# A new order in the tail of a mixture-of-experts kernel, and results scattered to their tokens

## The chip, the cores and the metric

The kernel runs on one core of one Trainium2 chip. A core has a matrix engine (TensorE, PE in the profile, with its weight loads as PEld), a vector engine (VectorE, DVE), a scalar engine (ScalarE, ACT), a general engine (GpSimd, POOL) and a queue engine (SyncE, SP), which issues most of the DMA transfers. Every engine works through its own list of instructions in order and waits for the others by semaphores. The metric is the device time of one execution, in microseconds (us). Three executions of the kernel before took 3097.17, 3097.98 and 3100.47 us; the median is 3097.98 us.

## The reference

Eight images of 256 channels and 32 x 32 pixels pass through two layers. The first is a deformable convolution-attention with a learned position bias. Its result is added to x. For the second, every image is a list of 1024 tokens of 256 numbers:

```python
t = _to_tokens(x)                                  # (8, 1024, 256)
n = _ln_t(t)
query = einsum('bnd,de->bne', n, q_weight)
t = t + einsum('bnm,bmd->bnd', sigmoid(einsum('bnd,bmd->bnm', query, n)), n)
tokens = _ln_t(t)
probs = softmax(tokens @ router_w.T)               # 8 experts
rw, re = top_k(probs, 2); rw = rw / rw.sum(-1)
out = tokens
for e in range(8):
    y = gelu(tokens @ w1[e] + b1[e]) @ w2[e] + b2[e]
    out = out + combine[:, e] * y                  # combine: rw where e is one of the two, else 0
x = _from_tokens(t + out)
```

All of it is in float32. The kernel computes only the two chosen experts of a token.

## The kernel before

The images, called batches here, run one behind the other. For each of them the main loop at L1118 makes 64 turns, which compute the position bias (three small layers, `first_layer`, `second_layer`, `third_layer`) and the softmax of the first layer. That work keeps PE busy for most of the kernel. The other work is written as Python generators. Every `yield` is a place at which the main loop goes on with something else, so the order of the instructions on each engine is the order in which the generators are advanced; `in_order` (L76) fixes it, except for the scatters at L793, which may move between the fixed POOL instructions on either side of them.

The generators of a batch are:

- `prep`: normalisation, offsets and sampling for the next batch.
- `attention` (L606): `upper` and `rest`. `rest` ends the softmax, forms the tokens `x1`, the normalised `tt` and `tn`, the queries (`to_query`), and then the sigmoid attention in `slots` (L714, with `ap`, `sg`, `vp`). `finish` normalises each pair of token tiles into `ut`, adds `ut` to `x1`, stores the sum in the memory tensor `xu`, and computes the router's logits.
- `route` (L812), from `rest`: the two experts of each token, their weights, and for each token and choice a row number, `slot`. Rows of one expert stand together and start at a tile border. A tile has 128 rows, in the last batch 256.
- The 16 scatters (L793): one indirect DMA for each of 8 token tiles and 2 choices writes rows of `ut` to the memory tensor `xs` at their `slot`. POOL issues them.
- `experts` (L911): per round, 256 rows. It fetches `xl` from `xs`, turns it with four transposes into `xg`, multiplies by the first weights (`hp`), applies Gelu (`ht`), multiplies by the second weights (`yp`), adds the bias into `yt` and stores that in the memory tensor `ys` (L951). The weights come by DMA from the expert number, which SP loads into a register (L931, L932). It has 12 rounds of two tiles for batches 0 to 6, with four weight loads a round, and 15 rounds of one tile for batch 7, with two.
- `combine` (L991), 22 steps: it fetches `xu` (`xc`), gathers for each token tile and choice the rows of `ys` at `slot` by an indirect DMA (`gs`, L1019), adds each gathered tile times its weight to `xc` (L1011), turns the sums back to channels (L1002, L1004) and stores them in `out` (L1005).

Tiles named by `low(...)` share 12 buffers, those by `psum(...)` two PSUM banks. In the main loop, `mix` decides when a third of a round of `experts` runs, for the batch two before the current one. After the last turn (L1175) the tail begins: `mains` holds the rest of batch 7's attention, `mixtures` the rounds of batch 6, `sums` the `combine` of batch 5. The loop is short:

```python
while mains:
    advance(mains)
    if sorted_ or not attending and n % 2:
        whole()
    sorted_ = sorted_ or sorting
    step(sums)
    n += 1
while mixtures:
    whole()
    step(sums)
```

`whole()` runs three steps, that is one round. `attending` holds while `slots` runs and while `route` runs, `sorting` while `route` runs. Batch 6's `combine` is appended to `sums` when its last round is done, and from there on it takes one step for each scatter of batch 7; what is left of it goes between batch 7's rounds. Batch 7's `combine` runs alone at the end.

Of the kernel before, what the change touches and what calls it, by code (L numbers as in the profile page):

```python
# [16 lines left out]
P = 128  # L17
# [14 lines left out]
def tiles_of(slots):  # L32
# [14 lines left out]
_CST = [  # L47
    ("ident", 128), ("gavg", 128), ("base", 128), ("basef", 128),
    ("gq", 1), ("cx", 1), ("cy", 8), ("rev", 8),
    ("one", 1), ("before", 128), ("full", 8), ("upto", E * E), ("tiles", TILES), ("form", 12),  # L50
]


# [50 lines left out]
def tile_conv_attn_hybrid(ctx: ExitStack, tc: tile.TileContext, x, par, qw, w1, w2_, cst, out):  # L104
# [118 lines left out]


    xss = [nc.dram_tensor(f"xs{n}", [ROWS, C], F32, kind="Internal").ap() for n in range(2)]
    power = cpool.tile([P, 8], F32, name="power")
    nc.vector.memset(power, -0.5)
    sents = set()
# [377 lines left out]
    def attention(b, st, o, rt):  # L606
# [66 lines left out]
        def finish(q):  # L673
            mv = tiny[q % 2][:, 0:4].rearrange("p (u s) -> p u s", s=2)
            for u in range(2):
                statistics(x1[:, 2 * q + u, :], mv[:, u, :])
            by = yield from factors(mv, 2)
            normalize(x1, ut, 2 * q, by)
            yield
            tp = psum("bp").rearrange("p (k i) -> p k i", k=2)  # L680
            for k in range(2):
                for u in range(2):
                    nc.tensor.transpose(
                        tp[:, k, u * P : (u + 1) * P], ut[:, 2 * q + u, k * P : (k + 1) * P], ident
                    )
            un = low("un")
            nc.scalar.copy(un, tp)
            uns.append(un)
            yield
            pair = slice(2 * q, 2 * q + 2)  # L690
            nc.gpsimd.tensor_tensor(x1[:, pair, :], x1[:, pair, :], ut[:, pair, :], ALU.add)
            nc.sync.dma_start(out=xu.rearrange("(m p) c -> p m c", p=P)[:, pair, :], in_=x1[:, pair, :])
            if q % 2:
                lq = psum("lq")
                for k in range(2):
                    for p_ in (q - 1, q):
                        nc.tensor.matmul(
                            lq[32 * p_ : 32 * p_ + 32, 0:Q], lhsT=rw[:, k, :], rhs=uns[p_][:, k, :],
                            start=(k == 0), stop=(k == 1), tile_position=(0, 32 * p_),
                        )  # L700
                rows = slice(32 * q - 32, 32 * q + 32)
                nc.scalar.copy(lqs[rows], lq[rows, 0:Q])
                yield
# [55 lines left out]
        def rest():  # L759
            nonlocal attending, sorting, ut, lqs  # L760
            for n, _ in enumerate(softmax(st, 1, 1, st["last"], o, psum)):
                if n == 1:
                    residual_bias(1)
                yield
            yield from to_query(1)
            ut = tokens("ut")
            lqs = low("lqs", (P, Q))
            attending = True

            for n, _ in enumerate(slots([(q, mp) for q in range(4) for mp in range(2 if q < 2 else 0, 4)], True)):  # L770
                if n % 3 == 0:
                    yield
                    others()
                yield
                others()
            attending = False
            while finishing:
                yield
                others()
            attending = sorting = True  # L780

            steps = route(lqs, rt, LARGE if b == NB - 1 else SMALL)
            for _ in range(5):
                while b < NB - 1 and turn % 2 == 0:
                    yield
                next(steps)
                yield
            attending = sorting = False

            xs, group = xss[b % 2], f"slots{b}"  # L790
            for n in range(16):
                m, c = divmod(n, 2)
                sent = nc.gpsimd.indirect_dma_start(  # L793
                    out=xs[:, :], out_offset=bass.IndirectOffsetOnAxis(ap=rt["slot"][:, c, m : m + 1], axis=0),
                    in_=ut[:, m, :], in_offset=None,
                )
                if n:
                    tc.declare_no_dep(sent.ins, group=group, reason="other slots")
                tc.add_to_no_dep_group(group, sent.ins)
                sents.add(sent.ins.name)  # L800
                if n == 1:
                    run(steps)
                yield
            rt.update(xs=xs, xu=xu)
            mixtures.append((b, experts(b, rt)))
# [105 lines left out]
    def experts(b, rt):  # L911
# [2 lines left out]

        several = LARGE // slots_
        rounds = -(-tiles_of(slots_) // several)
        yv = dram.tile([rounds * LARGE, C], F32, name=f"ys{slots_}")
        rows, tokens_, first, second = {}, {}, {}, {}

        def at(t):  # L920
            return slice(t * LARGE, (t + 1) * LARGE)

        def fetch(t):
            rows[t] = low("xl")
            nc.sync.dma_start(out=rows[t], in_=xs[at(t), :].rearrange("(s p) c -> p s c", p=P))  # L925

        def weights(t, pool, width, w, name):
# [11 lines left out]
        for n in range(rounds + 2):  # L939
            if n >= 2:  # L940
                f2, ht = second.pop(n - 2), tokens_.pop(n - 2)
                yp = psum("yp").rearrange("p (s c) -> p s c", s=2)
                for s in range(2):
                    for f in range(2):
                        nc.tensor.matmul(  # L945
                            yp[:, s, :], lhsT=ht[:, f, s * P : (s + 1) * P],
                            rhs=f2[:, s * several // 2, f * C : (f + 1) * C], start=(f == 0), stop=(f == 1),
                        )
                yt = low("yt")
                nc.vector.tensor_tensor(yt, yp, f2[:, 0:several, 2 * C :].to_broadcast([P, 2, C]), ALU.add)  # L950
                nc.sync.dma_start(out=yv[at(n - 2), :].rearrange("(s p) c -> p s c", p=P), in_=yt)  # L951
            if n == rounds + 1:
                break
            yield
            if n + 2 < rounds:
                fetch(n + 2)
            if n < rounds:
                second[n] = weights(n, w2pool, 3 * C, w2_, "w2")
            if 1 <= n <= rounds:
                f1, xg = first.pop(n - 1), tokens_[n - 1]  # L960
                hp = psum("hp").rearrange("p (f i) -> p f i", f=2)
                for f in range(2):
                    for u in range(several):
                        us = slice(u * slots_, (u + 1) * slots_)
                        for k in range(2):
                            nc.tensor.matmul(  # L966
                                hp[:, f, us], lhsT=f1[:, u, k * C + f * P : k * C + (f + 1) * P], rhs=xg[:, k, us],
                                start=(k == 0), stop=(k == 1),
                            )
                tokens_[n - 1] = ht = low("ht")  # L970
                for f in range(2):
                    for u in range(several):
                        us = slice(u * slots_, (u + 1) * slots_)
                        nc.scalar.activation(  # L974
                            ht[:, f, us], hp[:, f, us], AF.Gelu, bias=f1[:, u, 2 * C + f : 2 * C + f + 1]
                        )
            if n + 1 < rounds:
                first[n + 1] = weights(n + 1, w1pool, 2 * C + 2, w1, "w1")
            yield
            if n < rounds:  # L980
                xl = rows.pop(n)
                tp = psum("tp").rearrange("p (k i) -> p k i", k=2)
                for k in range(2):
                    for s in range(2):
                        nc.tensor.transpose(tp[:, k, s * P : (s + 1) * P], xl[:, s, k * P : (k + 1) * P], ident)  # L985
                tokens_[n] = xg = low("xg")
                nc.scalar.copy(xg, tp)  # L987
            yield
        sums.append((b, combine(b, rt, yv)))

    def combine(b, rt, yv):  # L991
        xu, slot = rt["xu"], rt["slot"]
# [125 lines left out]
    for n in range(NB * TURNS):  # L1118
# [9 lines left out]
        if b == 0 and i in (8, 16):  # L1128
            nc.sync.dma_start(
                out=xss[i // 8 - 1].rearrange("(t p) c -> p t c", p=P),  # L1130
                in_=zero.unsqueeze(1).to_broadcast([P, ROWS // P, C]),
            )
        if i == 46:
            residual(b)
        coming_ = (n // 8 + 1) * 16
# [37 lines left out]
            side.finish()  # L1173
    logits(total - 1)
    mains.append((b, below))  # L1175
    n = sorted_ = 0
    while mains:
        advance(mains)
        if sorted_ or not attending and n % 2:
            whole()  # L1180
        sorted_ = sorted_ or sorting
        step(sums)
        n += 1
    while mixtures:
        whole()
        step(sums)
    while sums:
        step(sums)
# [47 lines left out]
def _constants():  # L1236
# [14 lines left out]
        "full": np.broadcast_to(SMALL * np.arange(8.0)[None, :], (P, 8)),  # L1251
        "upto": np.broadcast_to((np.arange(E)[None, :] <= np.arange(E)[:, None]).reshape(1, E * E), (P, E * E)),
        "tiles": np.broadcast_to(np.arange(TILES)[None, :], (P, TILES)),


        "form": np.array(
# [40 lines left out]
```

## Time and profile before

| | |
|---|---|
| median of three runs | 3097.98 us (3097.17 to 3100.47) |
| the profiled execution | 3097.26 us |
| its span, first to last instruction | 3095.5 us |
| PE busy | 2814.5 us, 91% |
| PEld busy | 1391.9 us, 45% |
| DVE busy | 1932.1 us, 62% |
| ACT busy | 1872.0 us, 60% |
| POOL busy | 1381.3 us, 45% |
| DMA moved | 311.22 MB, mean 101 GB/s |
| mean granted TensorE clock | 0.976 |

The profile is of one execution. Busy times say how long an engine worked, not whether anything waited for it; the share over the whole span is a mean over the long main loop and a tail of about 300 us that looks quite different. A group's line gives the line of the code, the engine, the operation, the tiles written and read, and what ended the idle time before it in square brackets. SPq is SP's queue of DMA instructions, and the time of such an instruction is that of issuing it, not of the transfer.

### The profile page before, as it was taken

How to read it: one execution, taken by the hardware profiler on the slowest of the kernel's cores; microseconds unless marked ns; L12 is line 12 of the kernel's file. 1: busy time of each engine (PE TensorE's matmuls, PEld its weight loads, DVE VectorE, ACT ScalarE, POOL GpSimd, SP SyncE). 2: the span in 40 equal slices, each digit the busy share in tenths (PEclk: the TensorE clock that was granted, in tenths of full speed). 3: DMA queues.
4: the chain of work that ended last, by engine and by line, in shares of the span. 5: the costliest groups of instructions: out<-in, count | busy, mean ns of one | idle time of the engine just before them, and what ended most of it. 6: DMA issues, size and time to landing. Idle time of an engine off the chain costs nothing. (4 is left out here: it accounts for less than half of the span.)

```text
span 3095.5 us, 51726 instructions
## 1 busy us (share of the span) xinstructions
PE 2814.5 (91%) x19592; PEld 1391.9 (45%) x19592; DVE 1932.1 (62%) x2968; ACT 1872.0 (60%) x2715; POOL 1381.3 (45%) x945
## 2 busy tenths in 40 slices
PE   3889998899999999999999999999999999998845
PEld 2223443344454454544445444544545444446634
DVE  4887668766765677656865667656776565652211
ACT  3676656666666657666676666666566666663211
POOL 2555334643354544545535463545435454451131
PEclk7999999999999999999999999999999999999968
DMA  2321111111373125512364124731256331645556
GB/s 85 106 46 35 22 28 43 47 37 26 99 215 86 45 62 161 180 47 57 88 190 134 48 59 112 210 91 44 63 150 188 91 75 38 188 124 166 169 179 188
DMA packets 428297, 311.22 MB, mean 101 GB/s; under 512 B 284432, under 2 KB 368656, under 8 KB 428048
## 3 DMA queue, kind: packets, MB, share of 16 engines
q1 hardware_dynamic: 415472, 273.14, 31.5%
q0 software_dynamic: 12288, 33.57, 3.5%
q8 instruction: 155, 2.54, 0.3%
q10 hardware_dynamic: 288, 1.20, 0.1%
q14 instruction: 94, 0.77, 0.1%
HBM read 239.93 MB, written 67.90 MB: 99 GB/s over the span
## 5 line engine op out<-in xcount | busy, mean ns | idle before, releaser
L477 POOL TENSOR_TENSOR h<-ta,nb 128x1024 f32<-128x1024 f32 x512 | 980.8, 1918 | 1187.3 <-PE h2p L490 956.0
L490 PE MATMUL h2p<-h,pr__101 64*64 64x512 f32 x8192 | 1011.4, 606 | 59.6 <-DVE h L498 31.4
L496 ACT ACTIVATE h<-h2p,pr__101 128x1024 f32<-128x1024 f32 x512 | 570.4, 1114 | 537.1 <-PE h2p L490 535.6
L498 DVE TENSOR_TENSOR h<-h2p,nc 128x1024 f32<-128x1024 f32 x512 | 625.5, 1222 | 296.6 <-PE h2p L490 283.7
L475 DVE TENSOR_TENSOR h<-ta,still 128x1024 f32<-128x1024 f32 x512 | 620.1, 1211 | 28.8 <-ACT still L464 26.4
L482 ACT ACTIVATE h<-h 128x1024 f32<-128x1024 f32 x512 | 537.7, 1050 | 9.3 <-POOL h L477 9.1
L490 PEld LDWEIGHTS h2p<-h,pr__101 64*64 64x64 f32 x8192 | 254.0, 132 | 575.1 <-issue 286.6
L517 PE MATMUL sim<-h,pr__101 128*32 128x512 f32 x4096 | 493.4, 599 | 0.0
L950 DVE TENSOR_TENSOR yt<-yp,w 128x512 f32<-128x512 f32 x99 | 68.5, 692 | 352.8 <-PE yp L945 312.4
L517 PEld LDWEIGHTS sim<-h,pr__101 128*32 128x32 f32 x4096 | 107.4, 109 | 361.5 <-issue 361.5
L723 PE MATMUL ap<-qt,tn 128*128 128x256 f32 x1024 | 251.0, 389 | 2.5 <-DVE x L745 1.0
L733 PE MATMUL vp<-tt,sg 128*128 128x256 f32 x1024 | 233.0, 381 | 3.5 <-ACT nc L459 3.3
L723 PEld LDWEIGHTS ap<-qt,tn 128*128 128x128 f32 x1024 | 184.9, 190 | 86.2 <-issue 41.7
L945 PE MATMUL yp<-w,ht 128*128 128x256 f32 x792 | 198.0, 394 | 21.4 <-ACT ht L974 8.1
L1019 POOL DMA_INDIRECT gs<-ys,slot x128 | 129.2, 1009 | 192.5 <-DMA xc<-xu 107.3
L966 PE MATMUL hp<-xg,w 128*128 128x128 f32 (+1 forms) x1464 | 202.0, 291 | 12.5 <-ACT xg L987 3.5
L733 PEld LDWEIGHTS vp<-tt,sg 128*128 128x128 f32 x1024 | 193.7, 190 | 36.5 <-ACT nc L459 5.0
L966 PEld LDWEIGHTS hp<-xg,w 128*128 128x128 f32 x1464 | 182.4, 193 | 54.0 <-issue 33.6
L745 DVE TENSOR_TENSOR x<-x,vp 128x512 f32<-128x512 f32 x64 | 44.0, 688 | 237.1 <-PE vp L733 237.1
L974 ACT ACTIVATE ht<-hp,w 128x128 f32<-128x128 f32 (+1 forms) x366 | 108.2, 376 | 133.3 <-PE hp L966 126.3
L741 ACT ACTIVATE sg<-ap 128x512 f32<-128x512 f32 x128 | 76.4, 597 | 160.4 <-PE ap L723 149.8
L945 PEld LDWEIGHTS yp<-w,ht 128*128 128x128 f32 x792 | 144.5, 193 | 56.5 <-ACT ht L974 13.7
(272 smaller groups left out, 2566.1 us busy)
## 6 DMA issues: line engine op xcount, KB each, us to landing
w<-in_w SPq DMA_DIRECT2D x183, 384.0 KB, 3.7
w<-in_w SPq DMA_DIRECT2D x183, 257.0 KB, 3.4
ta<-fd SPq DMA_DIRECT2D x128, 256.0 KB, 4.9
xl<-xs SPq DMA_DIRECT2D x99, 256.0 KB, 3.3
ys<-yt SPq DMA_DIRECT2D x99, 256.0 KB, 2.2
nb<-fd SPq DMA_DIRECT2D x128, 128.0 KB, 4.7
xb<-in_x SPq DMA_DIRECT2D x8, 1024.0 KB, 4.9
x<-in_x SPq DMA_DIRECT2D x8, 1024.0 KB, 7.5
```

What stands on the lines that cost most here:

```text
L475: nc.vector.tensor_tensor(h1, a, b, ALU.max)
L477: nc.gpsimd.tensor_tensor(h1, a, b, ALU.subtract)
L482: nc.scalar.activation(h1, h1, AF.Relu)
L490: nc.tensor.matmul(h2p[gs, r, :], lhsT=par_("w2")[rs, gs], rhs=h1[rs, g].rearrange("p y x -> p (y x)"), start=True, stop=True, tile_positi ...
L496: nc.scalar.activation(h2, h2p, AF.Relu, bias=par_("cb2"))
L498: nc.vector.tensor_tensor(h2.rearrange("p r (y x) -> p r y x", x=W), h2p.rearrange("p r (y x) -> p r y x", x=W), nc_.unsqueeze(3).to_broad ...
L517: nc.tensor.matmul(sim[32 * q : 32 * q + 32, :], lhsT=par_("z3")[:, 15 - m : 47 - m], rhs=h2s[2 * u + q // 2][:, q % 2, :], start=False, s ...
L723: nc.tensor.matmul(ap[:, u, :], lhsT=tn[:, k, m0 : m0 + P], rhs=qt[:, k, quarter(q)], start=(k == 0), stop=(k == 1),)
L733: nc.tensor.matmul(vp[:, i, :], lhsT=sgs[s][:, u, i * P : (i + 1) * P], rhs=tt[:, 2 * todo[n - 2 + s][1] + u, :], start=(s == u == i == 0) ...
L945: nc.tensor.matmul(yp[:, s, :], lhsT=ht[:, f, s * P : (s + 1) * P], rhs=f2[:, s * several // 2, f * C : (f + 1) * C], start=(f == 0), stop ...
L966: nc.tensor.matmul(hp[:, f, us], lhsT=f1[:, u, k * C + f * P : k * C + (f + 1) * P], rhs=xg[:, k, us], start=(k == 0), stop=(k == 1),)
L1019: nc.gpsimd.indirect_dma_start(out=got[m][:, c, :], out_offset=None, in_=yv[:, :], in_offset=bass.IndirectOffsetOnAxis(ap=slot[:, c, m : m ...
```

## The change

The change has three parts, all for the tail and the last batch.

In the tail's loop, rounds of batch 6 run at other steps: one step in three where attention is not running, one in nine where it is, and every step of `route`. After `route` the one-in-three rule holds again. `combine` of batch 6 no longer steps in this loop; only that of batch 5 does. In the loop that follows, `sums` takes two steps a round.

Batch 7's tokens carry a 257th number, the row at which their result is to be stored. For the first choice that is the number of the token, for the second the same plus 1024. `ut` has 257 columns in this batch; its last column is filled from new constants, and 1024 is added to it after the eight scatters of the first choice, which now all come before those of the second. The rows go to a memory tensor of their own, `xsl`. It is filled once, in batch 0, with zeros and, in the last column, with row numbers past the tokens, for the rows that no token takes.

Each round of batch 7 copies that column of its 256 rows into `ids`. Instead of storing `yt` in `ys`, it scatters `yt` with two indirect DMAs from POOL to `zs`, at `ids`. In place of `combine`, `add_up` reads the token sums and both choices' results in token order with 12 plain DMAs, four of them issued from ACT, then multiplies, adds, transposes and stores as before.

```diff
--- before.py
+++ after.py
@@ -47,7 +47,7 @@
 _CST = [
     ("ident", 128), ("gavg", 128), ("base", 128), ("basef", 128),
     ("gq", 1), ("cx", 1), ("cy", 8), ("rev", 8),
-    ("one", 1), ("before", 128), ("full", 8), ("upto", E * E), ("tiles", TILES), ("form", 12),
+    ("one", 1), ("before", 128), ("full", 8), ("upto", E * E), ("tiles", TILES), ("form", 12), ("token", 2 * N // P + tiles_of(LARGE) * LARGE // P),
 ]
 
 
@@ -223,6 +223,11 @@
 
 
     xss = [nc.dram_tensor(f"xs{n}", [ROWS, C], F32, kind="Internal").ap() for n in range(2)]
+
+    last_tiles = tiles_of(LARGE)
+    xsl = nc.dram_tensor("xsl", [last_tiles * LARGE, C + 1], F32, kind="Internal").ap()
+    zs = nc.dram_tensor("zs", [2 * N + last_tiles * LARGE, C], F32, kind="Internal").ap()
+    ids = cpool.tile([P, last_tiles, 2], I32, name="ids")
     power = cpool.tile([P, 8], F32, name="power")
     nc.vector.memset(power, -0.5)
     sents = set()
@@ -675,7 +680,7 @@
             for u in range(2):
                 statistics(x1[:, 2 * q + u, :], mv[:, u, :])
             by = yield from factors(mv, 2)
-            normalize(x1, ut, 2 * q, by)
+            normalize(x1, ut[:, :, 0:C], 2 * q, by)
             yield
             tp = psum("bp").rearrange("p (k i) -> p k i", k=2)
             for k in range(2):
@@ -688,7 +693,7 @@
             uns.append(un)
             yield
             pair = slice(2 * q, 2 * q + 2)
-            nc.gpsimd.tensor_tensor(x1[:, pair, :], x1[:, pair, :], ut[:, pair, :], ALU.add)
+            nc.gpsimd.tensor_tensor(x1[:, pair, :], x1[:, pair, :], ut[:, pair, 0:C], ALU.add)
             nc.sync.dma_start(out=xu.rearrange("(m p) c -> p m c", p=P)[:, pair, :], in_=x1[:, pair, :])
             if q % 2:
                 lq = psum("lq")
@@ -763,7 +768,11 @@
                     residual_bias(1)
                 yield
             yield from to_query(1)
-            ut = tokens("ut")
+            if b == NB - 1:
+                ut = t8.tile([P, 8, C + 1], F32, tag="t8", name="ut")
+                nc.vector.tensor_copy(ut[:, :, C], cst_("token")[:, 0:8])
+            else:
+                ut = tokens("ut")
             lqs = low("lqs", (P, Q))
             attending = True
 
@@ -787,9 +796,13 @@
                 yield
             attending = sorting = False
 
-            xs, group = xss[b % 2], f"slots{b}"
+            xs, group = xsl if b == NB - 1 else xss[b % 2], f"slots{b}"
             for n in range(16):
                 m, c = divmod(n, 2)
+                if b == NB - 1:
+                    c, m = divmod(n, 8)
+                    if n == 8:
+                        nc.vector.tensor_scalar(ut[:, :, C], ut[:, :, C], float(N), None, ALU.add)
                 sent = nc.gpsimd.indirect_dma_start(
                     out=xs[:, :], out_offset=bass.IndirectOffsetOnAxis(ap=rt["slot"][:, c, m : m + 1], axis=0),
                     in_=ut[:, m, :], in_offset=None,
@@ -914,14 +927,14 @@
 
         several = LARGE // slots_
         rounds = -(-tiles_of(slots_) // several)
-        yv = dram.tile([rounds * LARGE, C], F32, name=f"ys{slots_}")
+        yv = None if b == NB - 1 else dram.tile([rounds * LARGE, C], F32, name=f"ys{slots_}")
         rows, tokens_, first, second = {}, {}, {}, {}
 
         def at(t):
             return slice(t * LARGE, (t + 1) * LARGE)
 
         def fetch(t):
-            rows[t] = low("xl")
+            rows[t] = low("xl", (P, 2, xs.shape[1]))
             nc.sync.dma_start(out=rows[t], in_=xs[at(t), :].rearrange("(s p) c -> p s c", p=P))
 
         def weights(t, pool, width, w, name):
@@ -948,7 +961,16 @@
                         )
                 yt = low("yt")
                 nc.vector.tensor_tensor(yt, yp, f2[:, 0:several, 2 * C :].to_broadcast([P, 2, C]), ALU.add)
-                nc.sync.dma_start(out=yv[at(n - 2), :].rearrange("(s p) c -> p s c", p=P), in_=yt)
+                if b < NB - 1:
+                    nc.sync.dma_start(out=yv[at(n - 2), :].rearrange("(s p) c -> p s c", p=P), in_=yt)
+                for s in range(2 if b == NB - 1 else 0):
+                    sent = nc.gpsimd.indirect_dma_start(
+                        out=zs[:, :], out_offset=bass.IndirectOffsetOnAxis(ap=ids[:, n - 2, s : s + 1], axis=0),
+                        in_=yt[:, s, :], in_offset=None,
+                    )
+                    if n > 2 or s:
+                        tc.declare_no_dep(sent.ins, group="results", reason="other tokens")
+                    tc.add_to_no_dep_group("results", sent.ins)
             if n == rounds + 1:
                 break
             yield
@@ -983,10 +1005,38 @@
                 for k in range(2):
                     for s in range(2):
                         nc.tensor.transpose(tp[:, k, s * P : (s + 1) * P], xl[:, s, k * P : (k + 1) * P], ident)
+                if b == NB - 1:
+                    nc.vector.tensor_copy(ids[:, n], xl[:, :, C])
                 tokens_[n] = xg = low("xg")
                 nc.scalar.copy(xg, tp)
             yield
-        sums.append((b, combine(b, rt, yv)))
+        sums.append((b, combine(b, rt, yv) if b < NB - 1 else add_up(b, rt)))
+
+    def add_up(b, rt):
+
+        xu, got = rt["xu"].rearrange("(m p) c -> p m c", p=P), []
+        zv = zs[0 : 2 * N, :].rearrange("(c m p) d -> p c m d", c=2, p=P)
+        for q in range(4):
+            pair = slice(2 * q, 2 * q + 2)
+            xl, z0, z1 = low("xc"), low("z0"), low("z1")
+            nc.sync.dma_start(out=xl, in_=xu[:, pair, :])
+            nc.sync.dma_start(out=z0, in_=zv[:, 0, pair, :])
+            nc.scalar.dma_start(out=z1, in_=zv[:, 1, pair, :])
+            got.append((xl, z0, z1))
+        for q, (xl, *zc) in enumerate(got):
+            tp = psum("op").rearrange("p (k i) -> p k i", k=2)
+            for u in range(2):
+                for c in range(2):
+                    nc.vector.scalar_tensor_tensor(
+                        xl[:, u, :], zc[c][:, u, :], rt["w"][c][:, 2 * q + u : 2 * q + u + 1], xl[:, u, :],
+                        ALU.mult, ALU.add,
+                    )
+                for k in range(2):
+                    nc.tensor.transpose(tp[:, k, u * P : (u + 1) * P], xl[:, u, k * P : (k + 1) * P], ident)
+            ot = low("ot")
+            nc.scalar.copy(ot, tp)
+            nc.sync.dma_start(out=out[b].rearrange("(k p) h w -> p k (h w)", p=P)[:, :, quarter(q)], in_=ot)
+        yield
 
     def combine(b, rt, yv):
         xu, slot = rt["xu"], rt["slot"]
@@ -1130,6 +1180,12 @@
                 out=xss[i // 8 - 1].rearrange("(t p) c -> p t c", p=P),
                 in_=zero.unsqueeze(1).to_broadcast([P, ROWS // P, C]),
             )
+        if b == 0 and i == 24:
+            rows_ = xsl.rearrange("(t p) c -> p t c", p=P)
+            nc.sync.dma_start(
+                out=rows_[:, :, 0:C], in_=zero.unsqueeze(1).to_broadcast([P, last_tiles * LARGE // P, C])
+            )
+            nc.sync.dma_start(out=rows_[:, :, C], in_=cst_("token")[:, 2 * N // P :])
         if i == 46:
             residual(b)
         coming_ = (n // 8 + 1) * 16
@@ -1173,16 +1229,19 @@
             side.finish()
     logits(total - 1)
     mains.append((b, below))
-    n = sorted_ = 0
+    n = 0
+
+
     while mains:
         advance(mains)
-        if sorted_ or not attending and n % 2:
+        if sorting or (n % 9 == 4 if attending else n % 3 == 1):
             whole()
-        sorted_ = sorted_ or sorting
-        step(sums)
+        if sums and sums[0][0] < NB - 2:
+            step(sums)
         n += 1
     while mixtures:
         whole()
+        step(sums)
         step(sums)
     while sums:
         step(sums)
@@ -1251,6 +1310,7 @@
         "full": np.broadcast_to(SMALL * np.arange(8.0)[None, :], (P, 8)),
         "upto": np.broadcast_to((np.arange(E)[None, :] <= np.arange(E)[:, None]).reshape(1, E * E), (P, E * E)),
         "tiles": np.broadcast_to(np.arange(TILES)[None, :], (P, TILES)),
+        "token": P * np.arange(_CST[-1][1])[None, :] + p[:, None],
 
 
         "form": np.array(
```

## The prediction

> **What bounds the kernel now.** I read the page first, then the busy time by stage over the tail (everything after the last second-layer matmul of batch 7, at 2792 us), then that stretch in order of time, then the waits. Batch 7 cannot be overlapped with a later batch, so its tail is all latency. I write E6, E7 for the expert rounds of batches 6 and 7, C6, C7 for their `combine` steps.
>
> Columns below: from:to, length, then busy us (and instructions) of PE, PEld, DVE, ACT, POOL, then clock, DMA share, GB/s.
>
> ```profile
> 2842.00:2890.00 48.00, 45.66 (x220) 38.48 (x218) 8.22 (x25) 14.86 (x28) 6.52 (x9) 1.00 0.19 58
> 2890.00:2922.20 32.20, 25.65 (x158) 21.76 (x158) 10.59 (x41) 11.08 (x29) 2.17 (x3) 0.95 0.68 209
> 2922.20:2943.90 21.70, 15.51 (x88) 12.18 (x88) 3.54 (x7) 5.48 (x18) 2.97 (x3) 1.00 0.85 279
> 2943.90:2981.70 37.80, 2.73 (x8) 1.37 (x8) 6.35 (x13) 1.17 (x2) 26.51 (x28) 0.53 0.43 139
> 2995.90:3063.30 67.40, 57.92 (x281) 47.81 (x279) 10.85 (x17) 19.08 (x43) 0.00 (x0) 1.00 0.76 228
> 3063.30:3095.50 32.20, 5.42 (x16) 2.74 (x16) 7.49 (x16) 2.34 (x4) 15.34 (x16) 0.53 0.45 139
> ```
>
> The reader should see two stretches in which PE hardly works: 37.8 us before E7 (PE 2.7 us) and 32.2 us after it (PE 5.4 us). In both, POOL issues indirect DMAs and the rest waits. The timeline names the cause:
>
> ```profile
> 2921.77 0.24 DVE L894 CAST slot<-still 128x8 int32<-128x8 f32 x2
> 2924.85 0.96 POOL L793 DMA_INDIRECT xs<-ut,slot  x1 [0.30 <-issue]
> 2943.11 0.69 DVE L950 TENSOR_TENSOR yt<-yp,w 128x512 f32<-128x512 f32 x1 [4.51 <-PE yp L945]
> 2946.97 0.98 POOL L1019 DMA_INDIRECT gs<-ys,slot  x1 [21.16 <-DMA xc<-xu]
> 2948.26 0.99 POOL L793 DMA_INDIRECT xs<-ut,slot  x1 [0.31 <-issue]
> 2979.05 0.97 POOL L793 DMA_INDIRECT xs<-ut,slot  x1 [0.30 <-issue]
> 2981.72 0.87 SPq L925 DMA_DIRECT2D xl<-xs  x2
> 3062.55 0.69 DVE L950 TENSOR_TENSOR yt<-yp,w 128x512 f32<-128x512 f32 x1 [3.65 <-PE yp L945]
> 3091.37 0.58 ACT L1004 COPY ot<-op 128x512 f32<-128x512 f32 x1 [6.28 <-PE op L1002]
> ```
>
> Slots are known at 2922.0. Three of batch 7's 16 scatters go out, then the POOL queue holds C6's first gather, which sits 21.16 us until E6's last rows are in memory; after it 13 scatters and 13 gathers alternate, 1.28 us each. E7's first fetch comes at 2981.72. After E7's last `yt` (ends 3063.24), C7 begins with 16 gathers. The waits say the same (total, times, longest):
>
> ```profile
> POOL gs L1019 <- DMA xc<-xu: 103.9, 2, 82.7
> ```
>
> **What the Trainium skill says.** "DMA: Bandwidth & Descriptors", Anatomy of one DMA, puts about 2 us of fixed completion latency on a POOL-issued DMA; the trace agrees: scatters land in a median 2.5 us in the tail, gathers in 2.8. The same page, Issuing engines are not separate DMA queues: queues share 16 engines and interleave. That bears on laying C6 over E7; the shares above (0.76 beside 0.43) are the budget. Its Rules for kernel authors: a strided last dimension becomes one descriptor per element. That concerns the new token column; this trace has no such transfer.
>
> **The change part by part.** I followed both loops by hand, step for step.
>
> *Order of E6.* Before, steps 3, 5, 7, 9, 11 of the tail run a round (up to hp 3) ahead of the last attention block, two more run while it finishes, then one per routing step. After, steps 4, 7, 10 (to hp 1), then 13 and 22 inside the attention block, 31, then each routing step. Both have issued hp 0 to hp 9 when the slots are emitted, so this adds no PE work before the slots. It does put Gelu between Sigmoids: four more ACT table loads of 1.28 us (one at 2842.9, one at 2897.4 are shown) = 5.1 us of ACT. With only two PSUM banks in that pool I let 3 us reach PE, plus 1 us because two rounds fewer fill `to_query`. **+4** (0 to +8).
>
> *Scatters before C6.* C6 now starts only after the main generators. Scatters 0 to 7 follow at 1.28 us each: 2922.2 to 2932.4, landing near 2936. Then DVE adds N to `ut`'s last column. That instruction waits for those landings and stands on DVE behind E6's last `yt` (end 2943.8), which is later; nothing of E6 is behind it. E6's end itself is set by SP's weight issues (about 5.3 us a round of 4 loads), which do not move; five scatters more beside a DMA share of 0.85 cost **+1**. POOL resumes at 2944.4 (0.4 for add and semaphore); scatter 15 starts 7 x 1.28 later, 2953.4; plus the 2.67 us from 2979.05 to 2981.72, the fetch is at 2956.0 instead of 2981.7: **-25.7** (-28 to -18).
>
> *E7 with C6 over it.* Per round: two result scatters on POOL for one `ys` store on SP, an index copy on DVE (about 0.2 us, hidden under PE's 4.65), and for 11 rounds two C6 steps. POOL: 2 scatters + 2 gathers = 5.1 us against a round of 4.8 (67.4 us over 14 rounds), for eight rounds: lag 2.6 us, recovered when the gathers are over. PE: at most two output quarters more, 8 transposes of 0.15, 1.2 us. DMA: E7 keeps the engines busy 0.76; C6's share of 2943.9:2981.7 is 0.43 x 37.8 = 16.3 us for 5.25 MB, less 13 scatters of 128 KB, leaves 11 us. Over nine full rounds (43 us): 0.76 x 43 + 11 = 43.7, just full. Rows of 1028 bytes instead of 1024 add a little. SP gains: without `ys` it no longer waits for `yt` before fetching weights, and PE waited only 4.4 us for weights in E7. **+6** (0 to +15).
>
> *The end.* Before: 3063.24 to 3095.5 = 32.3. After: two scatters 2 x 1.28 and landing 2.7 = 5.3 us; then z0, z1 of the first quarter (512 KB) from SP and ACT at once: 0.4 + 2 + 1.6 = 4.0; the remaining 2.25 MB at about 320 GB/s (the E6 stretch at share 0.94 to 0.96 moved 305 to 311) end 7.0 later, at 16.3; last quarter's 4 DVE ops 1.95, transposes 0.9, copy 0.6, issue and landing 3.5 as before: 23.3 to 23.8. **-8.7** (-12 to -4). The first three xu loads do not help: SP holds later ones behind the first z0.
>
> *The third fill at i = 24 and the token column.* SP is free from 121.0 (it waits until 157.1 for a buffer), the DMA share from 130 to 150 is 0.00 to 0.01. The fill needs 13.9 us, as the two others; the column is 3,840 elements of 4 bytes, unpriced by the trace. The loads behind it at 157.3 are used about 22 us after issue (90.4 to 113.1 for the set before). So the column may take about 40 us unseen: **0** (0 to +3). If that cover were gone, all of the column's time would be paid. 46 more constant columns (24 KB): 0.1. `ut` column writes: 0.2, under PE work.
>
> *Sum:* 4 + 1 - 25.7 + 6 - 8.7 = -23.4. The profiled execution took 3097.26 (span 3095.5 and 1.8 around it): 3073.9. It lay 0.7 below the median of the runs: **3074.6**.
>
> **Rivals.**
> (B) E7 becomes DMA-bound. For: the sum above is 1.0 of 16 engines, and E6 at share 0.85 to 0.96 ran 5.3 to 6.3 us a round. Against: E6 has twice the weight loads. At 5.9 us for eleven rounds, +12, with ramp +14, and the end saving only 5: 4 + 1 - 25.7 + 14 - 5 = -11.7, 3086.
> (C) Slower: a gather-to-DVE loop sets E7's round. DVE's `yt` of round r stands behind products that need a gather queued behind the scatters of round r-2's `yt`: two rounds >= 2.56 + landing + 0.48 + 0.69. With 2.8 us that is 3.3 us a round, no bound. Without E7's growth the gain is 29.4; nine rounds must each grow 3.3, to 8.1, so it decides once landings reach 12.5 us. The tail's longest gather was 6.0; the longest scatter of the kernel 13.9, which would give 8.8 a round, +36: 3104.
> (D) The 4-byte column stalls the first batch: beyond 40 us it pays one for one and turns the sign at 64 us, 270 ns per element on each engine. Likeliest if slow: 80 us, 3114.
> (E) The order doesn't do what it says: scatters still end late because E6 itself slips by as much as C6 gave back, about 20 us. Nothing in SP's or PE's work supports it. About 3097.
>
> **How the numbers follow.** Chances: likeliest 0.71, B 0.16, C 0.06, D 0.03, E 0.04. The likeliest's own spread (the ends above in quadrature: about 12 up, 10 down) is 3063 to 3087. The range 3060 to 3092 holds it and B, and leaves out about 2 in 10: C, D, E and an edge of B and of the likeliest. No change means within 0.2%, 6 us, about what a measurement of this kernel can tell. Faster takes the likeliest and B bar a twentieth: 0.86; same 0.05 (E and B's edge); slower 0.09 (C, D).
>
> **What would show it.** Right: POOL with 8 scatters, a gap, 8 scatters and no gather among them; first fetch of E7 near 2960; E7 from first fetch to last `yt` 85 to 90 us (81.5 before) with DMA share about 0.9; last `yt` to the end about 24; extra table loads between the Sigmoids and slots near 2926. Wrong: gathers still between scatters; rounds over 6 us with DVE waiting for gathers; PE waiting for tables near 160 us; z loads landing long after 16 us from the last `yt`.

## The result and the profile after

The changed kernel took 3070.77 us (median of four runs, 3064.17 to 3072.48) beside 3098.34 us of the kernel before: a ratio of 0.9906, 95% interval 0.9889 to 0.9923. It is 0.9% faster; 3074.6 us was predicted, within 3060 to 3092. Its profiled execution took 3070.33 us, its span is 3068.6 us.

The busy time by stage over the changed kernel's tail, with the columns as before (from:to, length, busy us of PE, PEld, DVE, ACT, POOL, clock, DMA share, GB/s):

```profile
2929.40:2953.40 24.00, 17.37 (x92) 13.78 (x90) 3.51 (x8) 5.98 (x19) 7.76 (x8) 0.93 0.86 282
2953.40:2965.40 12.00, 0.00 (x0) 0.00 (x0) 0.11 (x2) 0.00 (x0) 8.87 (x10) 0.67 0.31 110
2965.40:2977.70 12.30, 8.39 (x29) 6.58 (x30) 1.03 (x3) 2.00 (x4) 0.75 (x1) 0.63 0.82 256
2977.70:3046.70 69.00, 59.46 (x289) 48.53 (x287) 17.79 (x43) 20.38 (x45) 41.18 (x42) 1.00 0.87 273
3046.70:3068.60 21.90, 5.42 (x16) 2.31 (x16) 7.41 (x17) 2.34 (x4) 1.92 (x2) 0.57 0.57 192
```

The stretch between E6's end and E7's first fetch is 12.0 us instead of 37.9. The end is 21.9 us instead of 32.3. E7 from its first fetch to its last `yt` takes 81.3 us, no more than before (81.5): its last 14 rounds, with POOL busy for 41 of 69.0 us and more DMA traffic, are 1.7 us longer than before (67.3), and its start is 1.9 us shorter (12.3 and 14.2). In order of time:

```profile
2929.11 0.24 DVE L907 CAST slot<-still 128x8 int32<-128x8 f32 x2
2938.50 0.96 POOL L806 DMA_INDIRECT xsl<-ut,slot  x1 [0.30 <-issue]
2952.74 0.69 DVE L963 TENSOR_TENSOR yt<-yp,w 128x512 f32<-128x512 f32 x1 [3.64 <-PE yp L958]
2953.35 0.17 DVE L805 TENSOR_SCALAR ut<-ut 128x8 f32<-128x8 f32 x1
2953.79 0.96 POOL L806 DMA_INDIRECT xsl<-ut,slot  x1 [14.33 <-DVE ut L805]
2962.63 0.96 POOL L806 DMA_INDIRECT xsl<-ut,slot  x1 [0.30 <-issue]
2965.38 0.87 SPq L938 DMA_DIRECT2D xl<-xsl  x2
3046.01 0.69 DVE L963 TENSOR_TENSOR yt<-yp,w 128x512 f32<-128x512 f32 x1 [3.65 <-PE yp L958]
3050.92 0.38 SPq L1023 DMA_DIRECT2D z<-zs  x1
```

No gather lies between the scatters. What is left is a hole of 14.33 us between scatter 7, issued at 2938.5, and scatter 8. The add to the token column stands on DVE behind E6's last `yt`, and the second eight scatters wait for it.

The next table compares all profiles. Each time is counted from the start of the last group of second-layer products, because the main loop alone ended anywhere from 2789.2 to 2795.4 us, also in kernels in which it is the same. The slots, E6's end and the last `yt` are the ends of the last instructions that write them; the fetch is the start of its issue.

| kernel | slots | E6's end | E7's first fetch | last `yt` | end of span | E7: fetch to last `yt` |
|---|---|---|---|---|---|---|
| before | 132.5 | 154.3 | 192.2 | 273.8 | 306.0 | 81.5 |
| changed | 137.5 | 161.5 | 173.5 | 254.8 | 276.7 | 81.3 |
| changed, again | 137.9 | 161.4 | 173.3 | 256.1 | 277.5 | 82.8 |
| combine deferred only | 133.9 | 157.2 | 157.9 | 240.9 | 272.1 | 83.0 |
| the same, again | 130.1 | 155.3 | 156.0 | 238.0 | 269.5 | 82.0 |
| changed, old rule for rounds | 134.1 | 160.0 | 172.2 | 255.4 | 276.8 | 83.2 |
| changed, own copy | 137.4 | 161.5 | 162.2 | 246.2 | 267.7 | 84.0 |
| the same, again | 137.4 | 164.8 | 165.5 | 249.9 | 271.3 | 84.4 |
| results scattered, tail as before | 132.7 | 155.5 | 194.2 | 273.6 | 294.9 | 79.4 |
| own copy and old rule | 134.2 | 167.7 | 168.4 | 259.0 | 280.3 | 90.6 |
| the same, again | 134.2 | 158.2 | 159.0 | 240.9 | 262.4 | 81.9 |
| deferred, rows of 257 | 134.2 | 167.8 | 168.5 | 250.1 | 280.8 | 81.6 |
| own copy, combine last | 134.9 | 168.9 | 169.7 | 247.3 | 293.3 | 77.7 |

### The profile page after: what moved, and what is told of

It reads as the page before. It is cut to its first block, busy times and chain, and to the rows that moved or that the text cites. A ratio compares the mean times of both kernels' runs of the same rounds, so it can differ in the third digit from the quotient of the medians.

```text
span 3068.6 us, 51770 instructions
## 1 busy us (share of the span) xinstructions
PE 2819.6 (92%) x19592; PEld 1394.2 (45%) x19592; DVE 1933.5 (63%) x2985; ACT 1876.9 (61%) x2719; POOL 1395.1 (45%) x959
## 5 line engine op out<-in xcount | busy, mean ns | idle before, releaser
L495 PE MATMUL h2p<-h,pr__101 64*64 64x512 f32 x8192 | 1011.7, 606 | 59.4 <-DVE h L503 31.2
L1069 POOL DMA_INDIRECT gs<-ys,slot x112 | 114.2, 1019 | 78.6 <-issue 26.7
```

The source lines that it names most:

```text
L495: nc.tensor.matmul(h2p[gs, r, :], lhsT=par_("w2")[rs, gs], rhs=h1[rs, g].rearrange("p y x -> p (y x)"), start=True, stop=True, tile_positi ...
L1069: nc.gpsimd.indirect_dma_start(out=got[m][:, c, :], out_offset=None, in_=yv[:, :], in_offset=bass.IndirectOffsetOnAxis(ap=slot[:, c, m : m ...
```

## The experiments

**One part alone: `combine` of batch 6 deferred.** The kernel before, with

```diff
-        step(sums)
+        if sums and sums[0][0] < NB - 2:
+            step(sums)
         n += 1
     while mixtures:
         whole()
         step(sums)
+        step(sums)
```

> The kernel before, with one change: combine of batch 6 starts only after the main generators and then takes two steps a round. Theory (the 13 scatters queued behind the gathers were the cost, and that alone): slots at 2922 as before, 16 scatters of 1.28 us in one run, the last landing at about 2944; first fetch of batch 7's rows 2945 to 2949 instead of 2981.7; its 15 rounds 81 to 88 us; end 32 us as before; span about 3062, ratio 0.989 (0.986 to 0.992), as fast as the changed kernel without its other parts. Rival (the rounds of batch 7 only bear the gathers over them because the ys store has left SP's queue): rounds of batch 7 over 92 us, ratio 0.992 or more.

Measured: ratio 0.9902 (0.9885 to 0.9919), 3069.5 beside 3101.0 us. The stretches from the slots on, columns as above:

```profile
2929.30:2952.50 23.20, 16.12 (x89) 12.17 (x88) 3.52 (x8) 5.71 (x19) 15.46 (x16) 1.00 0.95 335
2952.50:2953.30 0.80, 0.00 (x0) 0.00 (x0) 0.04 (x1) 0.00 (x0) 0.00 (x0) 1.00 0.00 0
3036.30:3067.50 31.20, 5.42 (x16) 2.73 (x16) 7.58 (x16) 2.34 (x4) 15.14 (x16) 0.55 0.48 144
```

All 16 scatters fit into the 23.2 us in which E6 finishes, and E7's first fetch follows E6's end by 0.7 us instead of 37.9. Its times on the clock are later than expected because this run's main loop ended at 2795.4 us; counted from there, the slots lie at 133.9 (132.5 before) and the fetch at 157.9. E7 takes 83.0 us, the end 31.2. The first theory stands: the place of the gathers in POOL's queue was the cost, and moving them alone is worth what the whole change is worth, within the intervals. The rival asked for over 92 us in E7 and falls.

**One part undone: the rule for batch 6's rounds.** The changed kernel, with

```diff
-        if sorting or (n % 9 == 4 if attending else n % 3 == 1):
+        if sorted_ or not attending and n % 2:
             whole()
+        sorted_ = sorted_ or sorting
```

> The changed kernel with the old rule for the rounds of batch 6 in the tail. Theory (the two rounds inside the attention block cost about 5 us by table loads and the loss of filler): one table load between the sigmoids gone, slots at about 2922 to 2925 instead of 2929.4, end of batch 6's rounds 4 to 6 us earlier, total 3 to 6 us faster than the changed kernel, ratio to the kernel before about 0.989. Rival (the spread of rounds is neutral, the 7 us are drift of the main loop and a lower clock): slots within 2 us of 2929, ratio 0.990 to 0.991.

Measured: ratio 0.9891 (0.9873 to 0.9909), 3067.8 us. Four table loads in the tail instead of eight, and the slots 3.4 us earlier, as the theory has it. But E6's end comes only 1.5 us earlier and the first fetch 1.3, and the span from the main loop's end is the same (276.8 and 276.7). So the rounds inside the attention block do delay the slots (about 4 us on average over all profiles of the table, while two profiles of one kernel differ by up to 3.8), and in the changed kernel this is not worth much, since E6's end, not the slots, releases the second eight scatters. The rival's premise, slots within 2 us of 2929, missed. The ratio is the one the theory named, but the intervals don't tell it from the changed kernel's, and the spans show no gain.

**The hole taken away: a second copy of the tokens.** The changed kernel, with a tile `ut2` that carries the second choice's row from the start:

```diff
+                ut2 = t8.tile([P, 8, C + 1], F32, tag="t8", name="ut2")
+                nc.vector.tensor_copy(ut2[:, :, C], cst_("token")[:, 8:16])
...
+            if ut2 is not None:
+                nc.vector.tensor_copy(ut2[:, pair, 0:C], ut[:, pair, 0:C])
...
-                    if n == 8:
-                        nc.vector.tensor_scalar(ut[:, :, C], ut[:, :, C], float(N), None, ALU.add)
...
-                    in_=ut[:, m, :], in_offset=None,
+                    in_=(ut2 if ut2 is not None and c else ut)[:, m, :], in_offset=None,
```

> The changed kernel with a second copy of the last batch's tokens that carries the second choice's row from the start, so that nothing is added to the column between the scatters. Theory (the 14.3 us for which POOL waits between scatter 7 and scatter 8 lie on the path): 16 scatters in one run, first fetch at about 2952 instead of 2965.4, PE with almost no gap after batch 6's last product, total 9 to 13 us faster than the changed kernel, ratio about 0.987. Rival (the wait is covered: batch 6's rounds end at 2953 anyway and eight more scatters in the stretch of full DMA engines push them later): gain of 4 us or less.

Measured: ratio 0.9881 (0.9862 to 0.9899), 3062.6 us. The first fetch comes 0.7 us after E6's end; in the profile E7 begins 11.3 us earlier than in the changed kernel, and 2.7 us of that go into longer rounds. In the medians the gain over the changed kernel is 8 us, less than the 9 to 13 that the theory named and twice what the rival allowed. The hole was on the path.

**The other part alone: results scattered, tail as before.** The changed kernel with both loops of the tail as in the kernel before.

> The changed kernel with both loops of the tail as before, so that combine of batch 6 steps between the scatters again; what is left of the change is the token column, the scattered results and add_up. Theory (the parts are separate): first fetch of batch 7 at 2981 to 2988, its rounds about 81 us, last yt to the end about 22 us instead of 32; total 5 to 10 us faster than before, ratio 0.997 to 0.998. Rival (the end is short only because combine of batch 6 is out of the way earlier, or the column's wait costs more than the end saves): ratio 0.999 or more.

Measured: ratio 0.9962 (0.9950 to 0.9975), 3089.3 us. The first fetch is at 194.2 (192.2 before), E7 takes 79.4 us, and last `yt` to the end 21.3 us. So reading the results in token order is worth about 11 us at the end. The gains of the parts don't add up in the changed kernel: from the main loop's end, deferring alone takes off 33.9 us (36.5 in a second profile) and this part 11.1, both together only 29.3. What goes missing is the hole in front of E7, which only the two together have (12.0 us where the deferred kernel has 0.7; in this run most of it hides behind the gathers), and the later slots. The total came out somewhat better than expected, since the end gained 11.0 us and E7 2.1, of which the later fetch took 2.0.

**Both, first time.** The changed kernel with the second copy and the old rule.

> The changed kernel with the second copy of the tokens and the old rule for the rounds of batch 6. Theory (batch 6's rounds between the slots and their end are bound by weight loads and full DMA engines, so earlier slots only widen the wait): slots 3 to 5 us after those of the kernel before, counted from the last product of the main loop, end of batch 6's rounds no more than 2 us earlier than with the new rule, total within 3 us of the second copy alone, ratio 0.986 to 0.989. Rival (the attention rounds' 5 us come through once the column's wait is gone): 4 to 6 us faster than the second copy alone, ratio 0.985 to 0.986.

**Wider rows.** The kernel with `combine` deferred, and rows of 257 numbers for the last batch, the last one unused:

```diff
+                ut = t8.tile([P, 8, C + 1], F32, tag="t8", name="ut")
+                nc.vector.memset(ut[:, :, C], 0.0)
...
-            xs, group = xss[b % 2], f"slots{b}"
+            xs, group = xsl if b == NB - 1 else xss[b % 2], f"slots{b}"
...
-            rows[t] = low("xl")
+            rows[t] = low("xl", (P, 2, xs.shape[1]))
```

> The kernel before with combine of batch 6 deferred as in the first experiment, and the last batch's rows 257 numbers wide (the last one unused): scatters and fetches of 1028 instead of 1024 bytes, nothing else. Theory (the width costs little): slots to the end of batch 6's rounds 23 to 24 us as with 256 numbers (23.2), rounds of batch 7 83 to 84 us, total within 3 us of the first experiment. Rival [...]: slots to end 25 us or more, rounds of batch 7 86 us or more.

**`combine` of batch 6 after E7.** The second copy, with

```diff
     while mixtures:
         whole()
-        step(sums)
-        step(sums)
```

> The changed kernel with the second copy of the tokens, and combine of batch 6 after the last round of batch 7 instead of over its rounds. It measures what combine costs batch 7's rounds. Theory (the rounds are bound by PE, and combine over them costs 3 to 5 us, not the 6 to 15 that was allowed): first fetch to last yt 79 to 80 us instead of 84.0, DMA share in the full rounds about 0.7; the whole 20 us or more slower than with combine over the rounds. Rival (result scatters alone keep the engines full and combine is free): 83 us or more.

These three ran as one set, `combine` last with two executions, and each shows something that no other profile does. In the last of them:

```profile
2928.78 8.47 SPq L947 DMA_DIRECT2D w<-in_w  x4
2934.97 2.74 PE L960 MATMUL yp<-w,ht 128*128 128x256 f32 x8 [3.21 <-issue]
2944.28 0.96 POOL L808 DMA_INDIRECT xsl<-ut,slot  x1 [0.30 <-issue]
2947.92 0.69 DVE L965 TENSOR_TENSOR yt<-yp,w 128x512 f32<-128x512 f32 x1 [17.86 <-remote]
2948.13 1.14 ACT L998 ACTIVATE ht<-hp,w 128x128 f32<-128x128 f32 x4 [8.84 <-remote]
```

PE's product for `yt` ended at 2937.7, yet DVE began 10 us later, for no releaser that the profile knows (it writes `remote`; the 17.86 us before DVE's `yt` include the wait for the product). SP's four weight issues stretch over 8.47 us; in the round before it is 4.05. ACT stood too. The standstill lies over the run of scatters, which starts at 2925.2 and ends at 2945.2, and has passed 5 us after its end. E6's end comes 33 to 34 us after the slots; in all other profiles that is 22 to 27. Measured in this set: both, 0.9896 (0.9879 to 0.9912), 3071.7 us; wide rows, 0.9903 (0.9887 to 0.9920), 3072.2 us; `combine` last, 0.9942 (0.9922 to 0.9962), 3085.1 us.

In the first of the three it comes back inside E7. Its waits with that name over the whole execution (total, times, longest):

```profile
DVE yt L965 <- remote: 23.0, 2, 18.5
ACT ht L998 <- remote: 18.6, 3, 8.8
```

One wait of DVE (4.6 us) and two of ACT (4.9 each) lie in E7, which takes 90.6 us there and 81.9 in a second profile of the same kernel. In the other two profiles E7 has no such wait. So from this set only the E7 of these two is used. With rows of 257 numbers E7 takes 81.6 us, no more than with 256 (83.0, 82.0): the width costs E7 nothing that shows here. What it costs beside full DMA engines is hidden by the standstill and stays open. The experiment on `combine` is clear:

```profile
2972.50:3037.40 64.90, 57.02 (x273) 46.89 (x271) 10.62 (x27) 17.91 (x41) 26.85 (x28) 1.00 0.79 234
```

Without C6 over them, E7's last 14 rounds take 64.9 us, 4.64 each, and E7 77.7 us instead of 84.0. So C6 costs the own copy's rounds about 6 us (one profile without it), and saves far more: with C6 behind E7, last `yt` to the end is 46.0 us instead of 21.5. The theory's 79 to 80 us were a little too long, its DMA share of 0.7 too low. The median is 22.5 us above the first one of the own copy, as forecast, but in another set of runs.

**Once more, four kernels on one chip.** To see whether the standstill belongs to these kernels:

> The changed kernel itself, beside its variants on one chip. Ratio 0.990 to 0.991, slots to the end of batch 6's rounds 24 us, PE idle for 12 us between that end and the first fetch.

> The changed kernel with the second copy of the tokens, once more. In three kernels with 16 scatters in one run, SP, ACT and DVE stood still for 8 to 18 us while the scatters were issued, in two others with as many they did not. Theory (it belongs to that run of scatters beside full DMA engines, and falls in some executions): seen here or not, but if seen the first fetch is 7 us later than 2954 counted as before and the gain over the changed kernel 2 to 4 us instead of 8. Rival (it is a matter of that one chip or that one placement of code): not seen, ratio 0.988.

> The kernel before with combine of batch 6 deferred, once more. Ratio 0.989 to 0.991; whether the standstill is seen in the run of 16 scatters, with rows of 1024 bytes, is the question: theory sometimes, rival never.

> The changed kernel with the second copy and the old rule for the rounds, once more, beside the second copy alone. Theory: within 3 us of it. If the standstill is tied to this order of code, it is seen here again and this kernel is 5 us or more behind the second copy alone.

Measured, beside 3096.4 us of the kernel before: the changed kernel 0.9910 (0.9890 to 0.9930), 3069.4 us; own copy 0.9882 (0.9863 to 0.9901), 3061.6 us; deferred only 0.9890 (0.9868 to 0.9913), 3062.4 us; own copy and old rule 0.9872 (0.9847 to 0.9896), 3056.8 us. The standstill is in none of these profiles, though the last kernel is the same as `both` above, and the own copy is the same as `combine` last up to E7. In the last kernel, the same stretch without it:

```profile
2926.95 0.24 DVE L909 CAST slot<-still 128x8 int32<-128x8 f32 x2
2946.46 0.96 POOL L808 DMA_INDIRECT xsl<-ut,slot  x1 [0.30 <-issue]
2951.98 0.91 SPq L940 DMA_DIRECT2D xl<-xsl  x2
```

So the order of code doesn't cause it by itself. Nor does the chip: the set with the standstill and the first four experiments, which show none, ran on the same one. The other executions of `both` in that set (3069.14 to 3073.10 us) were 2 to 6 us faster than the profiled one; whether they stood still too isn't known. What causes it is open.

The deferred kernel is 7.0 us faster here than the whole change in the medians (3060.11 to 3068.54 beside 3067.26 to 3071.73), and 4.6 to 8.0 us shorter from the main loop's end in all profiles of the two. The intervals of the ratios overlap, but the pieces agree: the 10 us that the token column gains at the end are less than the 11.3 us of its hole and the later slots together. In the first set, though, the deferred kernel (3069.5 us) and the changed kernel with the old rule (3067.8) lay level, so that moving `combine` alone is the faster is not settled. What is shown is that the rest of the change, as it stands, gains nothing that can be told over moving `combine`; with the second copy the medians are 6.8 and 0.8 us below it in the two sets.

Own copy and old rule is the fastest version found: 12.5 us below the changed kernel in the medians of this set, and 4.7 below the own copy alone. That is more than the 3 us of the theory and within the 4 to 6 of the rival of its first experiment, but the intervals overlap. In its profile slots and E6's end come 3.2 and 3.3 to 6.6 us earlier than with the own copy alone, and the fetch follows E6's end by 0.7 us in both; that the earlier slots are worth something once the hole is gone fits this, but is not shown.

## Why the prediction was right

The changed span is 26.9 us shorter; 23.4 were predicted. By the steps of the sum, from the two profiles:

| step | predicted | measured | from |
|---|---|---|---|
| main loop | 0 | +2.4 | its end at 2791.9 instead of 2789.5 |
| order of E6, up to the slots | +4 | +5.0 | 137.5 - 132.5 |
| E6 from the slots to its end | +1 | +2.2 | 24.0 - 21.8 |
| E6's end to the first fetch | -25.7 | -25.9 | 12.0 - 37.9 |
| E7 with C6 over it | +6 | -0.2 | 81.3 - 81.5 |
| last `yt` to the end | -8.7 | -10.4 | 21.9 - 32.3 |

*Scatters before C6.* Right, in mechanism and size: eight scatters, a hole until E6's last `yt`, eight more, fetch 2.75 us after the last one's start (2.67 had been taken). The deferred `combine` alone shows that the gathers' place was the cause, and the second copy that the hole was a cost of the change and not of the kernel.

*Order of E6.* Right in kind and near in size: four table loads more, and PE waited 2.4 us for `ht` ahead of the sigmoid's products. How the 4 us divide between the loads and the missing rounds wasn't measured. Over all profiles with the old rule the slots lie at 130.1 to 134.2, with the new one at 134.9 to 137.9. I put the whole delay on the path; the old rule in the changed kernel gave back only 1.3 us at the first fetch. It was right for the changed kernel's slots but not all of it reached the end.

*E7 with C6 over it.* This is the term that was mis-sized, by 6 us (by 5 in the second profile of the changed kernel, 82.8 us). The DMA sum behind it came out: just full over 43 us was predicted, and from 2980 to 3020 us the share was 0.95 to 1.01. But the rounds hardly grew for it. That the total came out 3.5 us from the sum is in part luck: this term's 6.2 us too much stand against 4.6 us too little in the first three steps.

Two experiments split the term. In the deferred kernel C6 lies over E7 and the `ys` store is still there; with the results scattered and the tail as before, the store is gone and only C6's last steps (two gathers) lie in E7, as before. Their rounds after the first:

```profile
2966.20:3036.30 70.10, 59.63 (x289) 48.43 (x287) 16.14 (x31) 20.40 (x45) 11.85 (x12) 1.00 0.82 261
2997.80:3063.80 66.00, 57.96 (x281) 47.72 (x279) 11.82 (x30) 19.12 (x43) 26.89 (x28) 1.00 0.78 234
```

All of E7 takes 83.0 us in the deferred kernel and 82.0 in its second profile, so laying C6 over E7 costs 0.5 to 1.5 us against 81.5. With the results scattered it takes 79.4, so that part gives 2.1 us back. Together that is -1.6 to -0.6, near the -0.2 that was measured (+1.3 in the second profile of the changed kernel). So the cost of C6 was put too high, and the scattered results, which free SP of the `ys` store (named in the prediction, but left out of its sum), gave back about 2 us. POOL's full list does not set the growth: the deferred kernel's rounds grow as much with POOL busy for 11.85 of 70.1 us. The larger figure for C6 above, about 6 us, is against an E7 with no C6 at all, while E7 before already bore its last steps.

In the kernel before, SP's queue waited for `yt` in E7, in the queue's own waits (engine, line, waited for: total, times, longest):

```profile
SPq L951 <- DVE yt L950: 15.0, 11, 3.1
```

That wait stood ahead of the next weight loads. PE's wait for weights in E7 is 4.4 us with the store (5.4 and 4.4 in the deferred kernel), 1.9 with the results scattered and 0.9 in the changed kernel. That the shorter wait gave the 2 us fits these numbers, but the store was not taken away by itself.

*The end.* Right in kind: the first z load is issued 4.2 us after the last `yt` (5.3 expected), the last product ends 16.8 after it (18.3 expected), the rest is as expected. From the start of the last scatter to that load it is 2.67 us, as had been taken; the prediction counted this from the end of the second scatter's 1.28 us instead of its start. For the remaining loads it took about 320 GB/s where the rates it cites are 305 to 311, a slip of a few tenths of a us.

*The third fill and the token column.* Hidden, as argued. The column, for which the trace before had no price, has one now. SP's queue in batch 0:

```profile
121.66 1.01 SPq L1185 DMA_DIRECT2D xsl<-zero  x1
122.71 9.92 SPq L1188 DMA_DIRECT2D xsl<-cs  x1
157.81 0.58 SPq L448 DMA_DIRECT2D ta<-fd  x1
```

The issue alone takes 9.92 us. DMA engines are busy until about 142 us, and the loads behind come at 157.8, 0.7 us after their old time, as all loads from 91 us on do. So both were done about 16 us before the next load was even issued. The page counts 3,984 more packets under 512 bytes than before, about one for each of the column's 3,840 elements. The main loop's 2.4 us lie within its own spread: with no change in it at all, the deferred kernel ended its loop at 2795.4 and at 2791.1.

*The range.* The ends of the terms in quadrature come to about 14 us up and 8 down, not 12 and 10; the measured time lies well inside either way.

*The rivals.* (B) did not come: E7's DMA share was 0.87 over its full rounds and up to 1.01 in single stretches of 10 us, but the rounds took 4.93 us, not 5.9. (C): gathers landed in a median 4.7 and at most 5.7 us in E7, far from the 12.5 at which it would decide; DVE did wait 19.6 us for them in eight places, and POOL's list was full for a while, 5.13 us a round. (D) and (E) did not come.

## What to carry to other kernels

In a tail, look at who stands behind whom in the queue that issues gathers and scatters: the last of 16 scatters started 57 us after the slots were known, instead of 19, because one gather ahead of 13 of them waited for another stage's end, and moving it alone was worth 1%. When data is changed in place between two groups of transfers, the second group waits for the first to land and for all that stands ahead of the change on its engine; here a second copy gave back 8 us in all, although E7 was 1.2 to 3.1 us longer with it. Two parts of a change that each pay alone need not pay together: deferring `combine` and the token column are worth no more than deferring alone, until the column's hole is gone. A store that waits for its data in the queue that also prefetches can hold up the prefetch: the part that took it away made E7 2.1 us shorter.

## What the runs showed of the hardware that was not expected

The transfer of 3,840 single 4-byte elements took SP 9.92 us to issue, while the fill of the same 3,840 rows with 1,024 bytes each took 1.01 us.

In one set of runs SP, ACT and DVE stood still during a run of 16 scatters from POOL: DVE began 10 us after its data was ready, beside a DMA share of 0.97 to 1.01 at first and 0.5 to 0.8 later. In one of them it came back in E7. In five other profiles with as many scatters in one run it did not show. The standstill is shown, its cause is not.

With C6 over E7 the DMA engines' share was 0.95 to 1.01 for 40 us, and the 14 rounds of 69.0 us were only 1.7 us longer than at a share of 0.76.
